# Summing VectorE's scan products over a unit before one matmul adds them to the other states

## The chip, the cores and the metric

The kernel runs on one core of a Trainium2 chip. Its metric is the device time of one execution in microseconds, given as the median of three runs. Everything is float32. The core has five engines with queues of their own: TensorE (PE; its weight loads are listed apart as PEld), VectorE (DVE), ScalarE (ACT), GpSimd (POOL) and SyncE (SP), which here only issues DMAs. Each engine runs its own instructions in order and waits on semaphores for the others. In this kernel TensorE's results go to PSUM banks of 128 x 512, and GpSimd works on SBUF alone.

## The reference

Four layers follow one another on a tensor of 8 images x 64 channels x 64 x 64: attention over pixels with a depthwise convolution (layer 0), two blocks of 8 x 8 window attention with an MLP (layer 1), a filtered convolution (layer 2), and a state-space block (layer 3). The change lies in the selective scan of layer 3. Cut to that:

```python
def step(h, inp):
    u_t, dt_t, B_t, C_t = inp
    h = h * jnp.exp(dt_t[..., None] * A) + dt_t[..., None] * B_t[:, :, None, :] * u_t[..., None]
    return (h, jnp.einsum('bkcn,bkn->bkc', h, C_t))
...
_, ys = jax.lax.scan(step, h0, (u, dt, Bl, Cl))
return jnp.moveaxis(ys, 0, -1) + D[None, :, :, None] * xs
```

There are k = 4 directions, c = 128 channels, n = 16 states, and a scan of 4096 positions for each image, direction, channel and state. The last line of `step` is what the change touches: at every position the 16 states, each times its C, are summed to one y. Afterwards the four directions are added.

## The kernel before

The images go in four pairs. While the scans of one pair run, other work is dealt out beside them step by step, in proportion to a cost that each piece declares (`scans`, L1644): the front part of the next pair (layers 0 to 2 and the inputs of the scan) and the back part of the pair before (output norm, projection, the last mixing block). For the first pair most of the next front's layer 0 was already done; beside the last pair there is only a back part. After all four pairs the last back part runs alone.

The scan of a pair is cut into 64 **units**: 2 images x 4 directions x 8 pieces of 512 positions. A unit has eight **steps**, and a step handles two of the 16 states, 128 channels in the partitions and 512 positions along the row. For a step i:

- `fetch` (L1702) issues two DMAs on the SP queue that spread two rows of B and two of C over 128 partitions (tiles `B` and `C`, three buffers each), B three steps ahead and C two steps ahead.
- `products` (L1709), two steps ahead, lets GpSimd form B times dx for both states into the tile `vd` (L1712; six buffers).
- `step` (L1714): for each of the two states ScalarE writes exp(dt A) into a PSUM bank `dad` (L1732; three banks, tag `da`), VectorE scans along the 512 positions (L1735), and ScalarE copies the last column to `carry` (L1743) for the next piece. The products with C go back into `vd`. In even steps of the first three pairs GpSimd multiplies both states in one instruction (L1746). In odd steps, and in all steps of the last pair, GpSimd multiplies the first state (L1748), and the second state, which VectorE scanned in place in the PSUM bank, is multiplied by VectorE itself (L1749).
- `sums` (L1751), one step behind: two matmuls with the identity add both halves of `vd` into the PSUM bank `yd` (L1762; one bank, 16 matmuls to a unit). After the eighth step VectorE takes `yd` out: L1771 for the first direction, L1773 for the second and third (both into the SBUF tile `Y`), L1776 for the fourth, into a tile `yo` that a DMA stores (L1777).

Every float32 matmul stands in the trace as two records, so 16 matmuls of a unit are 32 records. `inputs` (L1678) prepares a unit ahead: it loads the piece of the input into `xs` (L1684; two buffers), makes dt, dx (`du`) and the rows of B and C.

The order in which each engine's instructions stand is not written by hand: a scheduler lays them out when the kernel is built, from the program's order and the dependencies, and a buffer that is to be used again makes its next writer wait for its last reader. The `behind` in `sums` only puts the first matmul of a step behind GpSimd's product of the next step in that layout.

Of the kernel before, what the change touches and what calls it, by code (L numbers as in the profile page):

```python
# [9 lines left out]
F32 = mybir.dt.float32  # L10
AF = mybir.ActivationFunctionType
ALU = mybir.AluOpType
# [3 lines left out]
B, C, HH, WW = 8, 64, 64, 64  # L16
L = HH * WW
P = 128
# [5 lines left out]
DI, NST, RNK, KDIR = 128, 16, 4, 4  # L24
TD = 512
# [201 lines left out]
class _Net:  # L227
# [353 lines left out]
    def in_range(self, pool):  # L581

        nc, tc = self.nc, self.tc
        m = self.sums.shape[1] * 64
        m2 = m + 2 * 4 * NH
        n = m2 + B * KDIR * NTD
        sums = self.sums.rearrange("p a b c -> p (a b c)")
        ok = pool.tile([P, n], F32, name="ok", tag="ok")
        top = pool.tile([P, n], F32, name="top", tag="top")
        cnt = self.const.tile([P, 1], F32, name="cnt", tag="cnt")  # L590
        bad = self.const.tile([1, 1], mybir.dt.int32, name="bad", tag="bad")
        nc.vector.tensor_scalar(ok[:, 0:m], sums, 1e-28, None, ALU.is_gt)
        nc.vector.tensor_scalar(top[:, 0:m], sums, 1e28, None, ALU.is_lt)
        nc.vector.tensor_tensor(ok[:, 0:m], ok[:, 0:m], top[:, 0:m], ALU.mult)
        for i, test in enumerate((ALU.is_lt, ALU.is_gt)):
            ws = self.wsum[:, i].rearrange("p b c -> p (b c)")
            d = ok[:, m + 4 * NH * i : m + 4 * NH * i + 4 * NH]
            nc.vector.tensor_scalar(d, ws, (1e28, 1e-28)[i], None, test)
        nc.vector.tensor_scalar(
            ok[:, m2:n], self.esum.rearrange("p a b c -> p (a b c)"), 1e28, None, ALU.is_lt  # L600
        )
        nc.vector.tensor_reduce(cnt, ok, AX.X, ALU.add)
        with tc.tile_pool(name="psr", bufs=1, space=PSUM) as ps:
            pc = ps.tile([1, 1], F32, name="pcnt", tag="pcnt")
            nc.tensor.matmul(pc, lhsT=cnt, rhs=self.ones[:, 0:1], start=True, stop=True)
            nc.vector.tensor_scalar(bad, pc, P * n - 0.5, None, ALU.is_lt)
        return nc.values_load(bad[0:1, 0:1], min_val=0, max_val=1, skip_runtime_bounds_check_because="a comparison gives 0 or 1")
# [541 lines left out]
class _Direct:  # L1149
# [111 lines left out]
    def layer0(self, p):  # L1261
# [11 lines left out]
        with self.work("w0") as wk:  # L1273
# [38 lines left out]

            sums = net.sums[:, p]
            nc.vector.tensor_reduce(sums, parts, AX.X, ALU.add)
            rec = wk.tile([P, 2, 32], F32, name="rec", tag="rec", bufs=1)
            nc.vector.reciprocal(rec, sums)
# [397 lines left out]
    def step(self, i, st):  # L1714

        nc, w, net = self.nc, self.w, self.net
        wk, ps = self.sw, self.ps
        u = self.units[i // 8]
        k, c, at, CC, v = u["k"], u["c"], u["at"], st["C"], st["v"]

        n0, rp = 2 * (i % 8), i % 2 or u["image"] >= B - 2
        rev = k >= 2

        def along(t):
            return t[:, ::-1] if rev else t

        h = wk.tile([P, 2 - i % 2, TD], F32, name="hd", tag=f"h{i % 2}", bufs=1)
        hs = []
        for j in range(2):
            n = n0 + j  # L1730
            da = self.bank("dad", (P, TD), "da")
            nc.scalar.activation(da, u["du"][:, 0], AF.Exp, scale=net.As[:, k, n : n + 1])  # L1732
            first = 0.0 if at == 0 else self.carries[:, n : n + 1]
            to = da if rp and j else h[:, j]
            nc.vector.tensor_tensor_scan(along(to), along(da), along(v[:, j]), first, ALU.mult, ALU.add)  # L1735
            hs.append(to)
            if at < NTD - 1 and (rp or j):
                ends = h[:, :, 0] if rev else h[:, :, TD - 1]
                cs = self.carries[:, n0 : n0 + 2]
                if rp:  # L1740
                    ends = to[:, 0:1] if rev else to[:, TD - 1 : TD]
                    cs = self.carries[:, n : n + 1]
                nc.scalar.activation(cs, ends, AF.Copy)  # L1743

        if rp == 0:
            st["w"] = nc.gpsimd.tensor_tensor(v, h, CC, ALU.mult)  # L1746
        else:
            st["w"] = nc.gpsimd.tensor_tensor(v[:, 0], h[:, 0], CC[:, 0], ALU.mult)  # L1748
            nc.vector.tensor_tensor(v[:, 1], hs[1], CC[:, 1], ALU.mult)  # L1749

    def sums(self, i, st, after=None):  # L1751

        nc, w, net = self.nc, self.w, self.net
        wk, ps = self.sw, self.ps
        u = self.units[i // 8]
        k, c = u["k"], u["c"]
        if i % 8 == 0:
            u["y"] = ps.tile([P, TD], F32, name="yd", tag="y", bufs=1)
        y = u["y"]
        for j in range(2):  # L1760
            n = 2 * (i % 8) + j
            m = nc.tensor.matmul(y, lhsT=w["ident"], rhs=st["v"][:, j], start=(n == 0), stop=(n == NST - 1))  # L1762
            if after is not None and j == 0:
                net.behind(m, after)
        if i % 8 < 7:
            return

        yd = net.part(self.Y, k, c)
        yp = y.rearrange("p (a b) -> p a b", b=64)
        if u["nth"] == 0:  # L1770
            nc.vector.scalar_tensor_tensor(yd, self.img(u["x"]), net.dsum, yp, ALU.mult, ALU.add)  # L1771
        elif u["nth"] < 3:
            nc.vector.tensor_tensor(yd, yd, yp, ALU.add)  # L1773
        else:
            o = wk.tile([P, TD], F32, name="yo", tag="yo", bufs=1)
            nc.vector.tensor_tensor(self.img(o), yd, yp, ALU.add)  # L1776
            nc.sync.dma_start(u["out"][:, c * TD : (c + 1) * TD], o)  # L1777

# [155 lines left out]
```

## Time and profile before

| what | value |
| --- | --- |
| median of 3 runs (lowest to highest) | 13789.17 us (13784.27 to 13789.92) |
| time of the profiled execution | 13842.86 us |
| its span, from first to last instruction | 13841.1 us |
| mean granted TensorE clock | 0.875 |
| VectorE busy | 8419.5 us (61%) |
| GpSimd busy | 8170.1 us (59%) |
| scans run from about | 2214 to 13587 us |
| the four pairs of scans end at about | 4720, 8078, 11443 and 13587 us |

Busy shares are means over the whole span, and the stages differ: until 2214 us there are no scans, and after 13587 us only the last back part is left. So the profile is read by stretches between those marks. Idle time of an engine is listed with what ended it, for example "POOL vd L1712 <- PE yd L1762": GpSimd could not start its product because a `vd` buffer was still to be read by a matmul. The granted clock is a share of TensorE's full speed.

### The profile page before, as it was taken

To read this page: it belongs to the slowest core of one execution; us is meant where nothing else is said; L and a number is where in the kernel's file an instruction comes from. 1 tells how busy PE (TensorE), PEld (TensorE's weight loads), DVE (VectorE), ACT (ScalarE), POOL (GpSimd) and SP (SyncE) were. 2 spreads that over 40 slices of the span, in tenths; PEclk is the share of its full clock that TensorE was granted. 3 is DMA by queue.
4 is the path that set the end of the run, shared out by engine and by line. 5 is a ranking of instruction groups with operands and counts; after the bars stand their busy time and mean duration, and the time that the engine had idled before them with its cause. 6 is when DMAs were issued, how large, how long until landed. Compare 5 with 4: busy or idle time off the path is not lost. (4 is left out here: it accounts for less than half of the span.)

```text
span 13841.1 us, 141364 instructions
## 1 busy us (share of the span) xinstructions
PE 11209.6 (81%) x46358; PEld 4137.2 (30%) x46358; DVE 8419.5 (61%) x9763; ACT 7076.0 (51%) x15475; POOL 8170.1 (59%) x4111
## 2 busy tenths in 40 slices
PE   9999986888887679989888667997898767666665
PEld 2243322334232222224432222223443222222221
DVE  0121336777668773366666766337665777987875
ACT  5556514565536545555544545555554544454442
POOL 0000005888778755566666775547665688878982
PEclk9999977898898889998888788998888888888887
DMA  0000005666667754454554764335544577777882
GB/s 23 1 1 1 1 14 188 232 238 226 215 215 250 247 169 135 140 178 169 173 169 169 241 232 157 131 128 193 183 163 154 198 253 262 270 250 271 278 272 97
DMA packets 705785, 2383.41 MB, mean 172 GB/s; under 512 B 81092, under 2 KB 81220, under 8 KB 704012
## 3 DMA queue, kind: packets, MB, share of 16 engines
q1 hardware_dynamic: 681312, 2319.76, 49.3%
q10 hardware_dynamic: 23724, 54.50, 1.0%
q8 instruction: 367, 6.01, 0.2%
q14 instruction: 382, 3.13, 0.1%
HBM read 2271.18 MB, written 102.76 MB: 172 GB/s over the span
## 5 line engine op out<-in xcount | busy, mean ns | idle before, releaser
L1712 POOL TENSOR_TENSOR vd<-B,du 128x1024 f32<-128x1024 f32 x2048 | 4840.6, 2369 | 3889.7 <-DVE X L1352 2197.2
L1762 PE MATMUL yd<-vd,pack 128*128 128x512 f32 x8192 | 4637.8, 697 | 1386.2 <-POOL vd L1746 574.0
L1735 DVE TENSOR_TENSOR_SCAN hd<-dad,carry,vd 128x512 f32<-128x512 f32 x2464 | 3090.6, 1271 | 1024.6 <-ACT dad L1732 494.7
L1732 ACT ACTIVATE dad<-du,As 128x512 f32<-128x512 f32 x4096 | 2716.2, 680 | 1087.3 <-DVE hd L1735 761.8
L1762 PEld LDWEIGHTS yd<-vd,pack 128*128 128x128 f32 x8192 | 1633.4, 216 | 4072.9 <-issue 1829.8
L1746 POOL TENSOR_TENSOR vd<-hd,C 128x1024 f32<-128x1024 f32 x768 | 1811.9, 2359 | 1212.3 <-DVE hd L1735 618.7
L1748 POOL TENSOR_TENSOR vd<-hd,C 128x512 f32<-128x512 f32 x1280 | 1637.9, 1281 | 297.3 <-DVE hd L1735 217.9
L1302 ACT ACTIVATE e<-s 128x512 f32<-128x512 f32 x2048 | 1201.7, 592 | 1022.4 <-PE s L1296 1020.4
L1735 DVE TENSOR_TENSOR_SCAN dad<-dad,carry,vd 128x512 f32<-128x512 f32 x1120 | 1427.0, 1274 | 119.3 <-POOL vd L1712 79.4
L1296 PE MATMUL s<-X 64*128 64x512 f32 x4096 | 1325.4, 649 | 74.3 <-ACT e L1302 74.1
L1288 PE MATMUL po<-e,VT 128*64 128x512 f32 x4096 | 1197.7, 628 | 13.3 <-ACT e L1302 13.2
L1743 ACT ACTIVATE carry<-hd 128x1 f32<-128x1 f32 (+1 forms) x1792 | 357.7, 202 | 1222.9 <-DVE hd L1735 1218.5
L1749 DVE TENSOR_TENSOR vd<-dad,C 128x512 f32<-128x512 f32 x1280 | 859.7, 672 | 63.9 <-ACT carry L1743 54.0
L1296 PEld LDWEIGHTS s<-X 64*128 64x128 f32 x4096 | 360.1, 187 | 952.6 <-issue 786.1
L1450 PEld LDWEIGHTS w_av<-vals,w_e 64*64 64x64 f32 x16384 | 561.0, 147 | 196.4 <-issue 87.9
L1450 PE MATMUL w_av<-vals,w_e 64*64 64x9 f32 x16384 | 589.3, 208 | 25.5 <-ACT w_e L1440 25.4
L1435 DVE TENSOR_TENSOR w_e<-w_s,bias 128x512 f32<-128x512 f32 x512 | 329.5, 681 | 448.1 <-PE w_s L1423 447.6
L1735 DVE TENSOR_TENSOR_SCAN hd<-dad,vd 128x512 f32<-128x512 f32 x352 | 419.5, 1210 | 174.1 <-ACT dad L1732 78.1
L1440 ACT ACTIVATE w_e<-w_e 128x512 f32<-128x512 f32 x512 | 311.6, 627 | 377.5 <-DVE w_e L1435 265.8
L1743 ACT ACTIVATE carry<-dad 128x1 f32<-128x1 f32 x1120 | 189.1, 169 | 602.5 <-DVE dad L1735 600.3
L1687 PE MATMUL pdd<-xs,xdt 128*128 128x512 f32 x512 | 338.7, 749 | 185.1 <-DVE hd L1735 72.4
L1288 PEld LDWEIGHTS po<-e,VT 128*64 128x64 f32 x4096 | 221.6, 136 | 824.5 <-issue 774.2
(247 smaller groups left out, 10798.1 us busy)
## 6 DMA issues: line engine op xcount, KB each, us to landing
B<-rows SPq DMA_DIRECT2D x2048, 512.0 KB, 5.0
C<-rows SPq DMA_DIRECT2D x2048, 512.0 KB, 4.5
xs<-xt SPq DMA_DIRECT2D x128, 256.0 KB, 3.2
xs<-xc SPq DMA_DIRECT2D x128, 256.0 KB, 3.6
xc<-xcv ACTq DMA_DIRECT2D x64, 256.0 KB, 3.7
zs<-z ACTq DMA_DIRECT2D x64, 256.0 KB, 4.3
xt<-XT ACTq DMA_DIRECT2D x32, 512.0 KB, 7.1
rows<-bc SPq DMA_DIRECT2D x256, 64.0 KB, 2.0
```

The lines of the kernel that those rows point to most:

```text
L1288: nc.tensor.matmul(po[half[im]], lhsT=VT[:, t, half[im]], rhs=es[im], start=(t == 0), stop=(t == 31))
L1296: nc.tensor.matmul(ss[im], lhsT=at(half[im], t), rhs=X[half[im], jc * CH : (jc + 1) * CH], start=True, stop=True)
L1302: nc.scalar.activation(e, ss[im], AF.Exp, scale=C**-0.5, accum_out=parts[:, im, t, jc : jc + 1])
L1450: nc.tensor.matmul(self.av[half[im], x % 4 + j, h, :], lhsT=es[h // 4][half[im], j, h % 4, :], rhs=V[half[im], x + j, h, :], start=True, s ...
L1712: self.nc.gpsimd.tensor_tensor(v, st["B"], dx.to_broadcast([P, 2, TD]), ALU.mult)
L1732: nc.scalar.activation(da, u["du"][:, 0], AF.Exp, scale=net.As[:, k, n : n + 1])
L1735: nc.vector.tensor_tensor_scan(along(to), along(da), along(v[:, j]), first, ALU.mult, ALU.add)
L1743: nc.scalar.activation(cs, ends, AF.Copy)
L1746: st["w"] = nc.gpsimd.tensor_tensor(v, h, CC, ALU.mult)
L1748: st["w"] = nc.gpsimd.tensor_tensor(v[:, 0], h[:, 0], CC[:, 0], ALU.mult)
L1749: nc.vector.tensor_tensor(v[:, 1], hs[1], CC[:, 1], ALU.mult)
L1762: m = nc.tensor.matmul(y, lhsT=w["ident"], rhs=st["v"][:, j], start=(n == 0), stop=(n == NST - 1))
```

## The change

In odd steps of the first three pairs VectorE's product no longer goes into `vd` for a matmul of its own. The first such product of a unit goes into a new SBUF tile `ysum` (128 x 512, one buffer); each of the three later ones is multiplied in place in its PSUM bank and then added to `ysum`. In the eighth step one matmul adds `ysum` to `yd`. So a unit has 13 matmuls in place of 16. The last pair keeps its products as they were. The tile `yo` is gone, in all four pairs: the result of the fourth direction is written over the unit's input tile `xs` and stored from there.

```diff
@@ step
-            nc.vector.tensor_tensor(v[:, 1], hs[1], CC[:, 1], ALU.mult)
+            if u["image"] < B - 2:
+                self.gather(i, u, hs[1], CC[:, 1])
+            else:
+                nc.vector.tensor_tensor(v[:, 1], hs[1], CC[:, 1], ALU.mult)
+
+    def gather(self, i, u, h, c):
+
+        nc = self.nc
+        if "sum" not in u:
+            u["sum"] = self.sw.tile([P, TD], F32, name="ysum", tag="ysum", bufs=1)
+            nc.vector.tensor_tensor(u["sum"], h, c, ALU.mult)
+        else:
+            nc.vector.tensor_tensor(h, h, c, ALU.mult)
+            nc.vector.tensor_tensor(u["sum"], u["sum"], h, ALU.add)
@@ sums
-        for j in range(2):
+        srcs = [st["v"][:, 0], st["v"][:, 1]]
+        if "sum" in u and i % 2:
+            srcs[1:] = [u["sum"]] if i % 8 == 7 else []
+        for j, v in enumerate(srcs):
             n = 2 * (i % 8) + j
-            m = nc.tensor.matmul(y, lhsT=w["ident"], rhs=st["v"][:, j], start=(n == 0), stop=(n == NST - 1))
+            m = nc.tensor.matmul(y, lhsT=w["ident"], rhs=v, start=(n == 0), stop=(n == NST - 1))
...
-            o = wk.tile([P, TD], F32, name="yo", tag="yo", bufs=1)
+            o = u["x"]
             nc.vector.tensor_tensor(self.img(o), yd, yp, ALU.add)
             nc.sync.dma_start(u["out"][:, c * TD : (c + 1) * TD], o)
```

## The prediction

> **What bounds the kernel now.** I read the page's engine totals first, then the busy times cut at the ends of the scan units, then the costliest groups, then the waits inside one stage. Totals first:
>
> ```profile
> PE 11209.6 (81%) x46358; PEld 4137.2 (30%) x46358; DVE 8419.5 (61%) x9763; ACT 7076.0 (51%) x15475; POOL 8170.1 (59%) x4111
> ```
>
> No engine is full, so the answer must come by stage. The busy times by stretch, first of the first pair (three stretches), then of the second pair (six); the third pair repeats the second within 2%:
>
> ```profile
> core 0: us, PE busy (x) PEld busy (x) DVE busy (x) ACT busy (x) POOL busy (x), PEclk, DMA share, GB/s
> 2214.00:3439.00 1225.00, 1018.14 (x7115) 463.26 (x7114) 923.28 (x1060) 683.28 (x1376) 1064.42 (x519) 0.90 0.69 233
> 3439.00:4106.00 667.00, 563.42 (x1263) 199.53 (x1262) 461.73 (x494) 305.47 (x619) 519.88 (x255) 0.90 0.63 212
> 4106.00:4720.00 614.00, 430.11 (x744) 151.19 (x744) 481.52 (x531) 388.66 (x682) 515.96 (x252) 0.84 0.75 252
> ...
> 5179.00:6147.00 968.00, 881.05 (x2644) 251.75 (x2644) 433.59 (x439) 534.54 (x1484) 531.85 (x257) 0.95 0.43 145
> 6147.00:6951.00 804.00, 723.31 (x6474) 369.40 (x6474) 552.21 (x711) 454.43 (x869) 528.35 (x256) 0.87 0.52 177
> 6951.00:7412.00 461.00, 413.61 (x1033) 151.40 (x1028) 272.42 (x327) 191.31 (x368) 261.18 (x128) 0.86 0.46 156
> 7412.00:7810.00 398.00, 276.85 (x466) 95.68 (x464) 296.20 (x355) 242.29 (x403) 255.03 (x125) 0.78 0.61 207
> 7810.00:8078.00 268.00, 175.52 (x302) 58.77 (x302) 188.71 (x179) 118.31 (x257) 254.51 (x125) 0.85 0.74 259
> ```
>
> The reader is to see three kinds of stage. From 5179 to 7412 us (pixel attention, window attention, layer 2 beside the scans) TensorE is busy 90 to 91% and VectorE 45 to 69%: TensorE leads. In the first pair GpSimd leads (1064 of 1225 us, 87%) with TensorE at 83%. From 7412 us TensorE drops to 70% and VectorE is at 74% (the vector convolution runs there), and from 7810 us GpSimd stands at 95% with the scans alone. The last pair is not summed differently.
>
> Inside the first TensorE stage the waits say the same:
>
> ```profile
> ACT e L1302 <- PE s L1296: 160.8, 96, 5.0
> POOL vd L1712 <- PE yd L1762: 155.5, 34, 7.4
> ...
> DVE Y L1773 <- PE yd L1762: 118.1, 7, 26.1
> ```
>
> In these 520 us ScalarE, GpSimd and VectorE all wait for matmuls, VectorE up to 26 us for a unit's last one.
>
> **The change, part by part.** The prices are in these groups:
>
> ```profile
> L1762 PE MATMUL yd<-vd,pack 128*128 128x512 f32 x8192 | 4637.8, 697 | 1386.2 <-POOL vd L1746 574.0 <-POOL vd L1748 396.4 <-DVE Y L1773 145.0
> L1749 DVE TENSOR_TENSOR vd<-dad,C 128x512 f32<-128x512 f32 x1280 | 859.7, 672 | 63.9 <-ACT carry L1743 54.0 <-DMA C<-rows 8.1
> L1776 DVE TENSOR_TENSOR yo<-Y,yd 128x512 f32<-128x512 f32 x64 | 43.5, 680 | 60.1 <-PE yd L1762 60.1
> L1773 DVE TENSOR_TENSOR Y<-Y,yd 128x512 f32<-128x512 f32 x128 | 124.5, 973 | 525.2 <-PE yd L1762 525.0
> ```
>
> *Removed from TensorE.* 192 units (64 in each of three pairs) lose 3 of 16 matmuls: 576 matmuls, 1152 records. In the sum's own busy time by stage, 3/16 is: pixel attention 272.24 and 276.21 us in the second and third pair, so 51 + 52 = 103; window attention 295.44 and 297.85, so 55 + 56 = 111; layer 2 138.63 and 136.10, so 26 + 26 = 52; first pair 555.28 until 3439 us, so 104, and 275.74 until 4106 us, so 52; everything else in those pairs 1213 us, so 227. In all 649 us. How much reaches the end? Where TensorE leads, not all: in the attention stage its stream also stops for ScalarE's exponentials between the two records of a score. I let 0.7 through in pixel attention (72), 0.5 in window attention, where VectorE's bias add and ScalarE sit in the chain too (55), 0.7 in layer 2 (36), 0.15 in the first pair's GpSimd stage (16), 0.3 in its layer 2 (16), nothing elsewhere. Gain 195 us. These shares are my choice between the ends: 0.3 of the 266 us in the three leading stages (80 us) and all of it with half of the first pair's 156 (344 us).
>
> *Added to VectorE.* 576 adds, one operand in PSUM, one in SBUF. The nearest row is L1776, the same operation with the same operands: 0.680 us, 392 us in all. Upper end L1773, 0.973, whose view of Y is strided; `ysum` is not, so I take 0.680. The products stay 768; three quarters now write into PSUM. The scan prices that: it takes 1274 ns into `dad` and 1271 into `hd`, so 3 ns x 576, nothing. Where does the 392 us hide? In the TensorE stages VectorE has 31 to 55% idle, in the GpSimd-only stage 30%. Not covered: the convolution stages (7412 to 7810 us and its like in the third pair, the two stretches from 4720 and 8078 us, the 16 units from 4106 us), 48 units x 3 x 0.680 = 98 us; I let 0.35 reach the end, 34. In the first pair's other 48 units also 98 us; 0.15, 14. Together 48 us; ends 0 and 196.
>
> *A longer hold on a PSUM bank.* The bank of an odd step's second state was free after the product; now after the add. In VectorE's built order one scan usually stands between the two, so 1.27 + 0.67, about 1.94 us longer, 768 - 192 = 576 times: 1117 us of bank time. Queued behind it are ScalarE's exponentials (L1732), which already waited 296.5 us in 297 waits for L1749, and behind those VectorE's scans. Two of three banks stay, and a scan needs one for 0.68 + 1.27 us, so I let 1.3% through: 15 us. Ends 0 and 25% (280).
>
> *A new wait on `ysum`.* With one buffer, a unit's first product waits for the last matmul of the unit before. In the built order that product always stands after the take-out of `yd` (L1771 to L1776), which waits for the same matmul, so it adds no wait of its own. Before, the product stood ahead of that take-out in most units, so a bank is now also held through that wait; where the wait is long TensorE leads and scans are not what is late.
>
> *The store from `xs`.* 64 units, all pairs. The load of the next `xs` in that buffer waits on SP for the store (landing 2.4 us median) and the B and C loads queue behind it: at most 64 x 2.4 = 154 us of SP time. SP is early as a rule: it waits 2220.0 us for L1712 and 2438.7 for L1746 to free B and C. GpSimd, in turn, waited 268.2 us for B. I take 5; ends 0 and 154.
>
> *Order.* The built orders show GpSimd's instructions unchanged in number, and in the shifted window rows of the second and third pair three units each whose last `yd` matmul stands behind 146 to 184 more small matmuls. At 589.3 us for 8192 of them (72 ns each) that is up to 13 us six times, 80 at most; TensorE has work there, so 5.
>
> Sum: 195 - 48 - 15 - 5 - 5 = 122 us less. Against the profiled execution, 13842.86 - 122 = 13721; that execution lies 0.4% above the median, so the median becomes 13789 - 122 = **13667 us**, 0.9% less.
>
> A rule speaks against counting removed matmuls in full. The Trainium skill, "TensorE: Matmul & The Clock Gate", Part 1, says that TensorE's clock is halved by default and that only sustained activity releases it, so a thinner stream of matmuls could run slower. The granted clock here is 0.95 at 91% busy and 0.78 at 70%, which agrees, but also 0.90 at 83% (from 2214 us) against 0.87 at 90% (from 6147 us), which does not follow busy time alone. By the rule, a clock lower by 0.03 in window attention would give back 0.03/0.87 of 723 + 730 us, 50 us, and the sum would be 72 us less; by the rows I charge nothing.
>
> **The rivals.**
>
> *A. TensorE's time was cover, not bound.* For it: in most stages two or three engines are within 20% of each other, and "POOL vd L1746" keeps TensorE waiting 574.0 us. Then 80 us come through and 75 go back on VectorE and SP: 13784 us, no change. Against it: 90% busy where VectorE has 31 to 55% idle.
>
> *B. The bank hold decides, and the kernel is slower.* Place: `dad`, three banks, in the first pair and the convolution stages, where scans starve already (VectorE waits 572.8 us for L1732 in all). If 25% of the 1117 us comes through, 280 - 15 more than in the sum: 13667 + 265 = 13932 us. It outweighs the rest from 137 us on (12% of the hold). Against it: ScalarE is busy 51% and can refill two banks meanwhile.
>
> *C. TensorE's time comes through whole* where it leads: 344 - 73 = 271 us less, 13518 us. For it: three engines wait for it there. Against it: its own waits for ScalarE.
>
> *D. It doesn't do what it says:* the built order has 192 first products, 576 in-place ones, 576 adds and 13 matmuls a unit, so no chance is kept for that.
>
> **How the numbers follow.** The chances: forecast 0.52, A 0.20, B 0.13, C 0.15. A difference under 0.2% (28 us) can't be told from none. The forecast's own range is 13590 to 13750. Faster: the forecast nearly whole (0.50), C (0.15), a part of A (0.05): 0.70. No change: 0.13, most of A. Slower: B and the tails of the forecast and of A (0.02 each), 0.17. For 8 in 10 the range reaches to C's middle, 13500, and past A to the milder end of B, 13830.
>
> **What would show it.** Right: `yd` records fall by 1152 and its busy time by about 650 us; the stretch of pixel attention shortens by some 36 us in each of two pairs, window attention by 27; VectorE's busy time grows by about 390; the GpSimd-only stretches and the last pair stay. Adds near 0.68 us. Wrong: if TensorE stays as long in those stretches with more idle time, A holds; if waits of L1735 for L1732 and of L1732 for the add grow by hundreds of us, B; if adds take 0.97 us or more, VectorE's term was too small by 169 us.

## The result, and the profile after

| what | before | after |
| --- | --- | --- |
| median (12 runs each, lowest to highest) | 13812.15 us (13782.62 to 13855.51) | 13800.48 us (13771.33 to 13820.91) |
| ratio after to before, with its 95% interval | | 0.9995 (0.9981 to 1.0009) |
| span of the profiled execution | 13841.1 us | 13800.1 us |
| mean granted TensorE clock | 0.875 | 0.857 |

The change makes no difference that the measurement can tell. The forecast was 122 us less. The engine totals of the kernel after:

```profile
PE 10937.2 (79%) x45206; PEld 3968.5 (29%) x45206; DVE 8742.4 (63%) x10339; ACT 7077.0 (51%) x15484; POOL 8165.7 (59%) x4111
```

The reader is to see that the work did move as the change says: TensorE has 1152 records fewer (46358 before) and 272 us less busy time, VectorE 576 instructions and 323 us more, GpSimd the same 4111. So the work left TensorE and the time did not go down. The stretches between the ends of scan units tell where it went (columns as in the table of the prediction; the first four lines are the second pair's pixel attention, window attention, layer 2 and the vector convolution, the last two are the scans alone, in the second and in the third pair):

```profile
5172.00:6098.00 926.00, 846.66 (x2548) 234.65 (x2546) 459.83 (x488) 533.70 (x1483) 530.89 (x257) 0.94 0.44 151
6098.00:6903.00 805.00, 697.78 (x6372) 355.54 (x6375) 581.51 (x760) 453.53 (x870) 527.60 (x256) 0.86 0.53 177
6903.00:7357.00 454.00, 399.93 (x985) 143.82 (x981) 286.29 (x350) 190.56 (x367) 262.98 (x129) 0.85 0.46 158
7357.00:7752.00 395.00, 273.00 (x426) 91.00 (x424) 311.60 (x380) 249.88 (x411) 254.47 (x124) 0.74 0.62 212
7752.00:8048.00 296.00, 190.19 (x291) 61.09 (x290) 214.89 (x218) 127.92 (x273) 253.92 (x125) 0.78 0.71 241
11057.00:11349.00 292.00, 181.41 (x290) 57.91 (x289) 213.93 (x217) 127.73 (x273) 255.70 (x125) 0.82 0.73 247
```

Pixel attention took 926 us in place of 968 and layer 2 454 in place of 461: there the gain is seen; window attention took 805 in place of 804. But the scans alone took 296 us in place of 268, and there GpSimd, which stood at 95% before, stands at 86% with the same 254 us of work. All that the forecast charged that stretch was a share of the 5 us for the store from `xs` and of the 15 us for the bank hold. And its units are those of the fourth direction, the only one whose result is stored from `xs`. Stretches of eight units, from take-out to take-out, in us:

| fourth direction, eight units | before | after |
| --- | --- | --- |
| first pair, first and second image | 319.8, 313.7 | 350.9, 357.7 |
| second pair | 402.1, 267.9 | 392.0, 296.0 |
| third pair | 405.9, 269.2 | 400.7, 292.6 |
| last pair | 265.0, 265.4 | 274.9, 286.3 |
| sum | 2509 | 2651 |

That is 142 us more, though TensorE's saving lies in these units as well, and the other three directions are shorter together by 166 us (2899, 3086 and 2839 before; 2859, 3061 and 2738 after). The last pair's two stretches, whose products the change leaves alone, grew too. The tile `xs` in the two traces points to a cause (engines that sat idle until the input's DMA landed: us, times). Before:

```profile
  DMA xs<-xc: 45.9, 15
```

After:

```profile
  DMA xs<-xc: 147.0, 46
```

And this is the order of events, in the timeline of before, in two units of the fourth direction of the last image (start us, us, engine, line, operation; in brackets the idle time ahead of it and what ended it):

```profile
13453.99 0.67 DVE L1776 TENSOR_TENSOR yo<-Y,yd 128x512 f32<-128x512 f32 x1
13454.69 0.32 SPq L1777 DMA_DIRECT2D ys<-yo  x1
...
13456.04 0.42 SPq L1684 DMA_DIRECT2D xs<-xc  x1
...
13462.62 2.05 PE L1687 MATMUL pdd<-xs,xdt 128*128 128x512 f32 x2 [4.06 <-DMA xs<-xc]
...
13471.08 0.37 SPq L1684 DMA_DIRECT2D xs<-xc  x1
...
13491.85 0.67 DVE L1776 TENSOR_TENSOR yo<-Y,yd 128x512 f32<-128x512 f32 x1
...
13521.10 0.67 DVE L1776 TENSOR_TENSOR yo<-Y,yd 128x512 f32<-128x512 f32 x1
```

And in the timeline of after:

```profile
13406.30 0.68 DVE L1792 TENSOR_TENSOR xs<-Y,yd 128x512 f32<-128x512 f32 x1
13407.00 0.32 SPq L1793 DMA_DIRECT2D ys<-xs  x1
...
13409.51 0.32 SPq L1684 DMA_DIRECT2D xs<-xc  x1
...
13414.57 2.04 PE L1687 MATMUL pdd<-xs,xdt 128*128 128x512 f32 x2 [3.70 <-DMA xs<-xc]
...
13443.45 0.67 DVE L1792 TENSOR_TENSOR xs<-Y,yd 128x512 f32<-128x512 f32 x1
...
13446.21 0.32 SPq L1684 DMA_DIRECT2D xs<-xc  x1
...
13480.41 0.68 DVE L1792 TENSOR_TENSOR xs<-Y,yd 128x512 f32<-128x512 f32 x1
```

Before, the input buffer is free as soon as dx and the rows of B and C are made from it, so loads (L1684) can run ahead: the one at 13471.08 is issued 21 us ahead of the take-out of 13491.85, though the one at 13456.04 comes 2 us behind a take-out; units end 37.9 and 29.2 us apart in turn. After, the load of 13409.51 comes 3.2 us after the take-out and 2.5 us after the issue of its store, the next 2.8 us after its take-out, and with the load the whole chain behind it (dt, dx, rows, B, product, scan) is late: both units end 37 us apart. The table gives the median lead of the fourth direction in the second and third pair's stretches of scans alone, from the third unit of each on, worked out from the traces (us relative to the take-out of the unit that held the buffer before):

| event of the unit that takes the buffer over | before | after |
| --- | --- | --- |
| load of `xs` issued | -28.2 | +3.0 |
| first matmul on it | -3.8 | +8.7 |
| ScalarE's first step of dt (L1689 in both) | -2.4 | +10.7 |
| its first load of B | +12.9 | +17.9 |
| its first scan | +25.7 | +31.2 |

Before, two loads of three in these units are issued 27 to 62 us ahead of the take-out, and their units' first scans come 25.1 to 26.1 us behind it; the third load comes 2 us behind the take-out, and its first scan 28.1 to 30.1. After, every load comes 2.8 to 3.2 us behind the take-out, and the first scans 28.5 to 34.5. What this does to GpSimd, which leads there, and to SP's queue, is in the waits of the third pair's stretch (us, times, longest; L1700 stores the rows of B and C, from which the B and C loads behind it read). Before, 269 us long:

```profile
POOL vd L1712 <- DMA B<-rows: 4.0, 5, 2.0
...
SPq L1700 <- ACT bc L1698: 11.6, 3, 4.4
```

After, 292 us long:

```profile
POOL vd L1712 <- DMA B<-rows: 16.3, 12, 3.0
...
SPq L1700 <- ACT bc L1698: 36.4, 7, 8.7
```

GpSimd waits 12.3 us more for B. Idle time ahead of its products (L1746) that the profile gives no reason for grew by another 10.4 us (3.5 to 13.9), and the two come to the 23 us by which the stretch is longer.

So the two parts of the change pull against each other: the sums save, the store from `xs` takes it back. That was the theory for the experiments; the rival was that the saving had not come through at all (rival A of the prediction) or was eaten by VectorE's adds and the bank hold (rival B).

### The profile page after: what moved, and what is told of

Read it like the earlier page. It is cut to its first block, busy times and chain, and to the rows that moved or that the text cites. A ratio compares the mean times of both kernels' runs of the same rounds, so it can differ in the third digit from the quotient of the medians.

```text
span 13800.1 us, 139980 instructions
## 1 busy us (share of the span) xinstructions
PE 10937.2 (79%) x45206; PEld 3968.5 (29%) x45206; DVE 8742.4 (63%) x10339; ACT 7077.0 (51%) x15484; POOL 8165.7 (59%) x4111
## 5 line engine op out<-in xcount | busy, mean ns | idle before, releaser
L1778 PE MATMUL yd<-vd,pack 128*128 128x512 f32 x6656 | 4072.8, 739 | 1586.7 <-POOL vd L1746 793.4
L1746 POOL TENSOR_TENSOR vd<-hd,C 128x1024 f32<-128x1024 f32 x768 | 1809.4, 2356 | 1323.9 <-DVE hd L1735 889.3
L1778 PEld LDWEIGHTS yd<-vd,pack 128*128 128x128 f32 x6656 | 1365.4, 226 | 3972.4 <-issue 1534.9
L1450 PE MATMUL w_av<-vals,w_e 64*64 64x9 f32 x16384 | 594.4, 209 | 36.6 <-ACT w_e L1440 36.4
L1789 DVE TENSOR_TENSOR Y<-Y,yd 128x512 f32<-128x512 f32 x128 | 124.3, 971 | 502.8 <-PE yd L1778 502.6
```

The source lines that it names most:

```text
L1450: nc.tensor.matmul(self.av[half[im], x % 4 + j, h, :], lhsT=es[h // 4][half[im], j, h % 4, :], rhs=V[half[im], x + j, h, :], start=True, s ...
L1778: m = nc.tensor.matmul(y, lhsT=w["ident"], rhs=v, start=(n == 0), stop=(n == NST - 1))
```

## The experiments

Each kernel was timed in turn with the kernel before on the same chip; a ratio is to that, with its 95% interval. In the texts put on record, e2 is experiment 2 below and e4 is experiment 5.

**1. The store from `xs` alone.** The kernel before, with one line of the change:

```diff
-            o = wk.tile([P, TD], F32, name="yo", tag="yo", bufs=1)
+            o = u["x"]
```

> The kernel before with one part of the change alone: the result of the fourth direction is written over the input tile xs and stored from there; VectorE's products and the matmuls are as before. Theory 1 (the store from xs holds up the next unit's input load, and that gave back what TensorE saved): 100 to 190 us slower than before, with the eight-unit stretches of the fourth direction 20 to 45 us longer. Theory 2 (the longer PSUM bank hold and VectorE's adds gave it back): within 30 us of before.

Measured: 13959.20 us against 13795.73, ratio 1.0113 (1.0091 to 1.0134). By the ratio this line alone costs 156 us. Its two stretches of scans alone, with all 16 matmuls a unit:

```profile
7835.00:8130.00 295.00, 195.46 (x342) 67.02 (x341) 201.57 (x194) 130.58 (x277) 256.29 (x126) 0.86 0.72 245
11198.00:11493.00 295.00, 194.75 (x342) 66.46 (x342) 202.46 (x195) 130.64 (x277) 256.99 (x126) 0.87 0.72 245
```

They have the 292 to 296 us of after, the load of `xs` is again issued 3.2 us behind the take-out (median), and the fourth direction's sum is 2638 us (2509 before). The line also moves the built order: counted in the trace, the last `yd` matmul of units 25 to 27 in the second and third pair stands 106 to 184 small matmuls later than before, much as in after (142 to 182). That is not what costs: the stretch of those units takes 396 and 404 us, before 402 and 406.

**2. The change without the store from `xs`.** The fourth direction's result goes into the half of the last `vd` that the unit has read by then:

```diff
-            o = u["x"]
+            o = st["v"][:, 1]
```

> The changed kernel, with the result of the fourth direction written into the second half of the last step's vd buffer, which nothing reads any more, and stored from there; xs is free as early as before. Theory 1: 100 to 200 us faster than before (13600 to 13700). Theory 2: within 40 us of before.

Measured: 13636.86 us against 13795.73, ratio 0.9876 (0.9854 to 0.9897), by the ratio 171 us faster. The same stretches:

```profile
7661.00:7935.00 274.00, 173.94 (x253) 54.57 (x252) 199.38 (x204) 117.15 (x257) 255.12 (x126) 0.73 0.73 255
10953.00:11225.00 272.00, 171.06 (x254) 54.34 (x253) 199.35 (x202) 116.97 (x255) 254.61 (x125) 0.75 0.73 256
```

They are back at 272 and 274 us (268 and 269 before), the load of `xs` is issued 28.5 us ahead of the take-out again, and the fourth direction's sum is 2497 us. Experiments 1 and 2 do and undo the same line, and each gives the other's answer: 156 us lost, 171 us won, 15 us net where the change itself measured 0.9995, about 7 us.

**3. The store into `vd` by itself.** The kernel before with `o = st["v"][:, 1]`, so that what experiment 2 gained isn't due to the store's new place.

> The kernel before with one edit: the result of the fourth direction is written into the free half of vd and stored from there; VectorE's products and the 16 matmuls are as before. Control for e2. If e2 is faster by the fewer matmuls, this is within 30 us of before; if the place of the store gained something by itself, it is 50 us or more faster.

Measured: 13800.40 us against 13790.21, ratio 1.0009 (0.9997 to 1.0021): nothing.

**4. VectorE's part without TensorE's.** Experiment 2 with 16 matmuls a unit. In the first three odd steps the second matmul then adds the half of `vd` that holds B dx, not a product with C:

```diff
-            srcs[1:] = [u["sum"]] if i % 8 == 7 else []
+            srcs[1:] = [u["sum"]] if i % 8 == 7 else srcs[1:]
```

> e2 with 16 matmuls again: VectorE makes and adds its products as in the change, but in the first three odd steps of a unit a matmul adds the second half of vd, which there holds B dx and not the product. It shows what VectorE's part costs alone, against before. Theory 1: 0 to 80 us slower than before. Theory 2: 130 to 250 us slower.

Measured: 13830.08 us against 13795.73, ratio 1.0026 (1.0015 to 1.0038). The in-place products, adds and longer bank hold cost 34 us together when no matmul is saved, and leaving the matmuls out is worth 13830 - 13637 = 193 us between the medians (207 by the ratios). Two things blur these figures a little: the matmuls that read B dx no longer wait for VectorE's products, and the built order is a new one in each kernel.

**5. No adds.** Experiment 2 without the line of the add, so that the three later products of a unit are left out of its sum.

> e2 without the 576 adds: 13 matmuls, the three later products of a unit are made in place and left out of the sum. It shows what fewer matmuls are worth without VectorE's adds and without the longer bank hold. Theory 1: 0 to 60 us faster than e2. Theory 2: 130 to 250 us faster than e2.

Measured: 13730.41 us against 13795.73, ratio 0.9955 (0.9939 to 0.9970). That is 94 us slower than experiment 2, which does more work; no theory expected it. The loss lies in the second and third pair's window rows and the eight-unit stretches after them (32 to 40, 40 to 48, 48 to 56): 423.3, 472.0, 406.2 us in the second pair where experiment 2 has 403.3, 450.5, 394.5, and 423.3, 472.0, 409.3 in the third where it has 405.9, 451.4, 399.3. In the stretch just ahead of these its built order differs: in units 26 to 30 of those pairs the last `yd` matmul stands 190 to 258 small window matmuls earlier than in the kernel before. So taking a line out is no clean test here, since the scheduler lays everything out anew.

**6. Short adds.** Therefore the add was kept and made short, on 8 of its 512 columns (the rest of the sum is left out):

```diff
-            nc.vector.tensor_tensor(u["sum"], u["sum"], h, ALU.add)
+            nc.vector.tensor_tensor(u["sum"][:, :8], u["sum"][:, :8], h[:, :8], ALU.add)
```

> e2 with the 576 adds cut to 8 of 512 columns: the same instructions and dependencies, but almost no time on VectorE; the sum is left out for the other columns. e4, without any adds, was 94 us slower than e2, and in its built order the last yd matmuls of the window rows stand before 190 to 258 small matmuls that they follow in the kernel before; here they stand within 50. If the order made e4 slow, this is 0 to 80 us faster than e2. If adds between the scans help by themselves, whatever their length, it is within 30 us of e2. If it is VectorE's time in the adds that helps, it is as slow as e4 (about 13730).

Measured: 13635.85 us against 13806.85, ratio 0.9874 (0.9858 to 0.9891), no different from experiment 2. The add's group, in experiment 2 and then here (operation, out<-in, shapes, count | busy us, mean ns | idle time ahead):

```profile
L1762 DVE TENSOR_TENSOR ysum<-ysum,dad 128x512 f32<-128x512 f32 x576 | 382.6, 664 | 0.9
```

```profile
L1762 DVE TENSOR_TENSOR ysum<-ysum,dad 128x8 f32<-128x8 f32 x576 | 81.9, 142 | 1.2
```

Of 383 us of adds 301 were taken away, and the time stayed. So in sum the adds' duration costs nothing that can be seen here; the sum is what stayed, for the order is not the same, and the first direction's stretches together grew by 57 us while the fourth's shrank by 28. It was not VectorE's time in the adds that made experiment 2 faster than experiment 5. What did, the order or the adds' mere presence between the scans, the result doesn't tell, since it fits both expectations. The cause of those 94 us stays open.

**7. Bank hold against operands in SBUF.** Experiment 2 with the three later products written to `vd` and added from there, so that the PSUM bank is free after the product, as before:

```diff
-            nc.vector.tensor_tensor(h, h, c, ALU.mult)
-            nc.vector.tensor_tensor(u["sum"], u["sum"], h, ALU.add)
+            nc.vector.tensor_tensor(to, h, c, ALU.mult)
+            nc.vector.tensor_tensor(u["sum"], u["sum"], to, ALU.add)
```

> e2 with the three later products of a unit written into vd, as before the change, and added to ysum from there: the PSUM bank is free after the product again, but both operands of the add lie in SBUF. If the longer bank hold costs much (theory 2), this is 50 us or more faster than e2. If it doesn't, it is 20 to 150 us slower, because adds with both operands in SBUF take 1.2 to 1.5 us in the rows of before (1.47 us at L1856) and not 0.67.

Measured: 13937.07 us against 13790.21, ratio 1.0110 (1.0094 to 1.0126), 300 us slower than experiment 2 between the medians, twice the upper end of what was expected. The hold was shorter and the kernel far slower. The add now reads both operands from SBUF (groups by line, as above):

```profile
L1762 DVE TENSOR_TENSOR ysum<-ysum,vd 128x512 f32<-128x512 f32 x576 | 746.8, 1297 | 0.8
...
L1746 POOL TENSOR_TENSOR vd<-hd,C 128x1024 f32<-128x1024 f32 x768 | 1917.4, 2497 | 1252.8 <-DVE hd L1735 708.7 <-issue 440.0 <-DMA B<-rows 49.8
```

The add takes 1297 ns in place of 664, and GpSimd's product 2497 in place of 2353. Two operands in SBUF are not slow by themselves. In the kernel before, the add of L1856 reads both from SBUF; after 13600 us, when GpSimd has no products left, and then beside the last pair's products (11500 to 13580 us), it takes:

```profile
L1856 DVE TENSOR_TENSOR X<-X,ge 128x512 f32<-128x512 f32 x8 | 5.5, 686 | 0.1
```

```profile
L1856 DVE TENSOR_TENSOR X<-X,ge 128x512 f32<-128x512 f32 x8 | 12.4, 1555 | 0.0
```

The Trainium skill, "SBUF — State Buffer", section "Who interferes with whom", says that a VectorE instruction with two SBUF inputs contends with a GpSimd instruction that reads SBUF, and that one with at most one SBUF input, outside VectorE's 2-port modes, does not; these durations agree. So an add that keeps one operand in PSUM is what makes the change cheap. What a shorter hold is worth by itself this run can't say, since its dearer adds may hide it; that the hold costs little is shown by experiment 4, where hold, adds and products cost 34 us together.

**8. Releasing `xs` earlier.** If the lost lead is what costs, the first direction has the same fault in all kernels so far: its take-out (L1771 before) reads `xs` for D x. Experiment 2, with ScalarE writing D x into `Y` as soon as the input is there:

```diff
+        if u["nth"] == 0:
+            nc.scalar.activation(net.part(self.Y, k, c), self.img(x), AF.Copy, scale=net.dsum)
...
-            nc.vector.scalar_tensor_tensor(yd, self.img(u["x"]), net.dsum, yp, ALU.mult, ALU.add)
+            nc.vector.tensor_tensor(yd, yd, yp, ALU.add)
```

> e2, and in the first direction ScalarE writes D x into Y when the unit's input arrives, so that the take-out of the first direction no longer reads xs and that buffer too is free before the unit ends; 64 ScalarE activations of 128 x 512 more. If the unit's end as the last reader of xs is what delays the next input (theory 1), the eight-unit stretches of the first direction get shorter where the scans set the pace (272 us in the second image of the last pair, to about 250) and the whole is 30 to 120 us faster than e2. If only the store's landing matters, it is within 30 us of e2.

Measured: 13582.92 us against 13790.21, ratio 0.9852 (0.9838 to 0.9867), the fastest of all. Against experiment 2 that is 54 us between the medians and 33 by the ratios, whose intervals overlap, so the size is uncertain; the place is not: the first direction's sum falls from 2854 to 2777 us. The first direction of the last image, in experiment 2 and then here (columns as above):

```profile
12344.00:12616.00 272.00, 171.75 (x287) 58.50 (x286) 205.36 (x209) 118.16 (x279) 226.46 (x128) 0.82 0.76 262
```

```profile
12321.00:12566.00 245.00, 161.29 (x285) 56.80 (x284) 206.66 (x209) 122.80 (x286) 225.66 (x128) 0.86 0.85 285
```

The same GpSimd work in 27 us less. The first image's of the last pair went from 299.6 to 268.2 us. The second direction gave 28 us of it back (2972 to 3000).

## Why the prediction was wrong, point by point

**The step that failed is "The store from `xs`".** It was priced at 5 us, as the time that SP would wait for the store with the B and C loads queued behind it, with 154 us as its end. SP did not pay it as a wait for the store. In after, the waits of SP's queue in the third pair's stretch of scans alone list for the store (us, times, longest):

```profile
SPq L1684 <- DMA ys<-xs: 5.7, 6, 1.2
```

Its wait for the rows, which are late because the input is late, is what grew there (11.6 to 36.4 us, above). The price came from the buffer: `xs` has two of them, and a buffer that is written at the unit's end can't take the next-but-one input before that. What was lost was the load's run-ahead, 31 us in the median (from 28.2 us ahead of the take-out to 3.0 behind it), of which 5.5 reached the unit's first scan. The term should have been 156 us. That this is close to the upper end, 64 stores by 2.4 us, does not confirm that end's reason, which was SP's time. How much of the 156 belongs to the store's landing and how much to the take-out ahead of it, no run sets apart; the first direction, where a buffer waits for the take-out alone, cost less (experiment 8). "SP is early as a rule" was true of B and C, and said nothing of a load that has to wait for the take-out itself.

**Removed matmuls: the sum was right, its places were not.** Forecast 195 us; experiments 2 and 4 give 193 (207 by the ratios). From the stretches of experiment 2 against before, which hold VectorE's costs too: pixel attention 99.5 us in the two pairs (forecast 72, all there was 103), window attention 21 (55), layer 2 11 (36), the first pair's GpSimd stage 18 (16), its layer 2 44 (16); with 12 elsewhere that is the 206 us between the two profiled spans. Window attention and layer 2 gave a third of what was asked of them, though TensorE was 90% busy there; pixel attention gave nearly all that there was, and the first pair's layer 2 nearly three times its share. That the misses cancelled is luck. The sign named for it did not come: the busy time of the `yd` matmuls was to fall by about 650 us and fell by 342, all of TensorE's by 272, with the records as forecast (1152). The `yd` matmuls on `vd` that are left take 739 ns in the mean in place of 697.

**VectorE's adds and the bank hold: too dear.** They were priced at 48 and 15 us. Together they cost 34 with the matmuls kept (experiment 4), and shortening the adds brought nothing back with the matmuls gone (experiment 6). The add itself took 667 ns, forecast 680; the in-place product 680.

```profile
L1761 DVE TENSOR_TENSOR dad<-dad,C 128x512 f32<-128x512 f32 x576 | 391.5, 680 | 13.4 <-ACT carry L1743 12.4 <-DMA C<-rows 0.3
```

The signs named for rival B, waits that grow by hundreds of us, did not come either. In after ScalarE's exponentials wait 159.8 us for the add, 123.5 for the last pair's products and 56.2 for a unit's first product, 339.5 us together, where they had waited 296.5 us for the products before. The scans that write `hd` wait 557.2 us for them (572.8 before).

```profile
DVE hd L1735 <- ACT dad L1732: 557.2, 222, 12.1
...
ACT dad L1732 <- DVE ysum L1762: 159.8, 82, 6.4
```

**The wait on `ysum`** was priced at nothing, and that holds: in after, VectorE sits idle 3.6 us ahead of the 192 first products (L1759) in all, 3.5 of it for `carry`. A wait that the forecast did not name lies on the other side: TensorE sits idle 63 us ahead of the 384 records that read `ysum`, nearly all for the last add (L1762). Experiments 2 and 4 include it; no run sets it apart.

**The order** was priced at 5 us for window rows in which some last `yd` matmuls stand later. Experiment 1 shows that it is mostly the `xs` line that moves them, and that the stretch of those units is no longer for it.

**Rival A had the time, not the mechanism.** 13784 us was its figure (13782 with the sum's 73 us in place of its 75), and the result is 0.1% from it. But TensorE's time was no cover: it came through at 193 us. "The GpSimd-only stretches and the last pair stay" was the sign that spoke at once: they grew by 28 and 23 us (7752 and 11057 us) and by 9.9 and 20.9 us (last pair).

**The clock.** The prediction weighed whether a thinner stream of matmuls would run at a lower clock. Where TensorE leads it did in after by little: 0.95 to 0.94, 0.87 to 0.86, 0.86 to 0.85. The 50 us asked for 0.03 in window attention; it moved 0.01. The larger fall, from 0.85 to 0.73 in the scans alone (experiment 2), lies where GpSimd leads at 255 of 274 us, and cost at most the 3 to 6 us by which those stretches are longer than before.

## What to carry to other kernels

Before you reuse an input buffer for a result, count not the bytes nor the queue but the lead: ask when the buffer was free until now, when it is free after, and how long the chain is from the load that waits for it to the first instruction that needs it. Here two buffers and a store at the end of the unit cost 2.4 us a unit (156 us over 64 units), all but 15 us of what the saved matmuls of 192 units had brought. A change of several parts that measures as nothing is worth taking apart: with one line put right this one is 1.2% faster than the kernel before, and with the first direction's buffer released early too, 1.5%.

## What the runs showed of the hardware

Fewer matmuls did not make TensorE less busy where it was not the leader. In the scans alone, 302 records took 175.52 us before at a granted clock of 0.85, and 253 took 173.94 us in experiment 2 at 0.73, while experiment 1 with 342 records took 195.46 at 0.86. So in such a stretch TensorE's busy time is no measure of the work that was taken from it. Busy time times granted clock, an estimate of the work at full clock, is 0.49 to 0.50 us a record in all three: the work did fall with the records, and the lower clock filled the time again.

An addition of 128 x 512 on VectorE beside GpSimd's products took 664 ns with one operand in PSUM and 1297 with both in SBUF, while one with both in SBUF took 686 ns with GpSimd idle. Moving 576 adds from the one form to the other, in a built order that is new as well, made the kernel 300 us slower (experiments 2 and 7); the adds themselves took 364 us more and GpSimd's work 176 (8336.2 us in place of 8160.4), 110 of it in L1746.
